# A graph layer on one core: embedding columns inside the message products, features transposed, distances on four row groups

## The chip, the cores and the metric

The kernel runs on 1 core of one Trainium2 chip. The metric is device time in microseconds (us) of one execution. All data is f32.

## What is computed

The input is `x`, 32 graphs of 512 nodes with 256 channels, and `adj`, 32 masks of 512x512 zeros and ones. After a layer norm and a relu (`h`), one graph layer is applied and added to `x`:

```python
h = jnp.maximum(_layernorm(x), 0.0)
# convolution branch
hc = relu(bn1(conv1x1(h)));  x_conv = relu(bn2(conv17(hc)) + h)
# graph branch
s = h @ w_se.T + b_se                          # 3 numbers for each node
sq = jnp.sum(s * s, axis=-1)
dist = sq[:, :, None] + sq[:, None, :] - 2.0 * jnp.einsum('bnd,bmd->bnm', s, s)
A = jnp.exp(-dist) * adj
msg = relu(h @ w_msg.T + b_msg)                # 256 channels
x_nmp = jnp.einsum('bnm,bmd->bnd', A, msg)
# a gated unit on both branches
gi = concat([x_conv, x_nmp]) @ w_ih.T + b_ih;  gh = h @ w_hh.T + b_hh
r, z = sigmoid(gi_r + gh_r), sigmoid(gi_z + gh_z);  n = tanh(gi_n + r * gh_n)
out = x + (1 - z) * n + z * h
```

The change touches the graph branch alone: `s`, `dist` and `msg`.

## The kernel before

The kernel is written in a tile framework that orders the instructions of each engine itself, from the order in which the code issues them and from its own estimates; waits come from the tiles that instructions share. The order of the code therefore sets the order of the engines only roughly. Graphs are called b (0 to 31), in two groups of 16 (GB = 16). HT[b] is `h` of one graph with channels on the partitions, 128 x 2 x 512.

The program runs through these stages, with their place in the profiled execution:

- 0 to 249 us, "first" and "gen": layer norm, transposes (`phT`) and the 1x1 convolution (`pc`, L266) of graphs 0 to 15; the weights of the 17-tap convolution go to frequencies (`pw`, L216: products of 17 rows on four row groups of the array, each in its own PSUM bank). The weights of the graph branch and of the gates are fetched in `load_weights`, on ACT's DMA queue.
- 249 to 628 us, "nodes": the graph branch of graphs 0 to 15. In between lie 40 frequency products (`py`, L309), two for each even b and three for each odd b, two of them behind `affinity`, the third at the end of the pass.
- 628 to 735 us: "first" of graphs 16 to 31.
- 735 to 1390 us, "rest": gates of graphs 0 to 15, with the second 40 frequency products.
- 1390 us to the end, "nodes" and "rest" together: graph branch and gates of graphs 16 to 31. While the gates of graph b run, the graph branch of b + 1 is worked in between.

The graph branch of one graph consists of these functions:

- `embed`: `ps` (L329), a product of 96 weight columns with HT[b], computes the three numbers of each node three times, on partitions 0, 32 and 64. Four ACT instructions (L332 to L335) add the bias, double or square, and write the tiles `sl` and `sr` (96 x 512), of which 32 rows each hold a constant -1.
- `message`: `pm` (L345), 128 nodes by 256 channels for each of four chunks of nodes, two chunks to a bank; DVE adds the bias (L348), ACT takes the relu (L349).
- `affinity`: for each of four chunks a product `pd` (L357) of 96 rows, which gives -dist at once; ACT takes the exponential `e` (L359); PE transposes the mask into `pa` (L362); DVE multiplies both into `A` (L363).
- `aggregate`: `pn` (L371), the product of `A` and `msg`; DVE copies it out (L373).

The gates are `pg` with the sigmoid `rz` (L426), `pgh`, `pgi` (L411) and `n` (L438); `po` (L453) transposes back. Each matrix product of f32 is two instructions in the trace, and a transpose is one; all PSUM tiles come from one pool of eight banks. The loop of the last stage, in the code's order:

```python
load_nodes(b + 1); load_rest(b + 1, False)
embed(b + 1)
message(b + 1)
gates_rz(b)
affinity(b + 1)
gate_n(b)
aggregate(b + 1)
freq_to_windows(b + 1)
finish(b)
```

## Time and profile before

| | |
|---|---|
| runs | 2270.57, 2271.43, 2273.3 us; median 2271.43 us |
| the profiled execution | 2272.12 us, of which the span of the trace is 2270.3 us |
| granted TensorE clock, mean | 0.979 |
| busy: PE, DVE, ACT | 97%, 33%, 26% of the span |
| the 16 graphs of the "nodes" stage | 379 us |
| bytes moved | 308.89 MB, 136 GB/s on average |

Times in the profile are in us unless marked ns. PE is TensorE's matrix product, PEld its weight load, DVE VectorE, ACT ScalarE, POOL GpSimd, SP SyncE; SPq and ACTq are their DMA queues. A row of a group names its source line, engine, operation, what it writes and reads, the shapes and the count; behind the bar stand busy time and the mean of one in ns, then the idle time of the engine ahead of it and what ended it. In rows in order of time, the first number is the start and the second the time until the last of the row's instructions has ended; the ends of matrix products overlap the next one's start, so that their pace is read from start to start.

### The profile page before, as it was taken

The numbers are of one execution on the slowest core, as the hardware profiler recorded it, in microseconds if no ns is written. First come the engines' busy times: TensorE is split into PE (matmuls) and PEld (weight loads), VectorE is DVE, ScalarE is ACT, GpSimd is POOL, SyncE is SP. The second block draws the span as 40 slices with busy tenths as digits, with TensorE's granted clock in tenths as the row PEclk, the third lists the DMA queues.
The fourth block names the chain that finished last, engine by engine and source line by source line (L and its number), as shares of the span: only waits on it lengthen the run. The fifth ranks groups of instructions, "written<-read, shape, count | busy, mean of one in ns | idle before, by whom it ended". The sixth has DMA issues, their size and how long they took to land.

```text
span 2270.3 us, 20711 instructions
## 1 busy us (share of the span) xinstructions
PE 2197.3 (97%) x8000; PEld 1316.4 (58%) x8000; DVE 744.6 (33%) x1416; ACT 596.5 (26%) x946; POOL 93.0 (4%) x119
## 2 busy tenths in 40 slices
PE   5888999999999999999999999999999999999998
PEld 4556666666688555555555554555555555555554
DVE  5556422223277122321321222223322222222323
ACT  1333333333234211111111111322222322222221
POOL 1000100000011000000000000000000000000000
PEclk7888999999999999999999999999999999999999
DMA  7878665665554453464464443222222222222210
GB/s 207 275 228 264 202 235 197 221 217 198 199 190 153 119 181 118 148 194 126 129 187 132 147 143 81 71 75 64 73 64 76 78 73 64 64 64 64 64 37 19
DMA packets 207650, 308.89 MB, mean 136 GB/s; under 512 B 11713, under 2 KB 158145, under 8 KB 207553
## 3 DMA queue, kind: packets, MB, share of 16 engines
q1 hardware_dynamic: 193152, 272.93, 39.2%
q10 hardware_dynamic: 14401, 34.65, 4.1%
q8 instruction: 63, 1.03, 0.2%
q14 instruction: 34, 0.28, 0.0%
HBM read 202.68 MB, written 104.86 MB: 135 GB/s over the span
## 4 chain that ended last, share of the span: by engine, by line
PE 91%; DVE 4%; DMA 3%; issue 1%; POOL 1%; ACT 0%; SPq 0%; DVEq 0%; POOLq 0%; ACTq 0%
PE pg L411 29%; PE pgi L411 10%; PE pn L371 10%; PE py L309 9%; PE pc L401 5%; PE pd L357 5%; PE pgh L411 5%; PE pm L345 5%; PE pc L266 4%; PE pa L362 2%; PE ps L329 2%; PE px L280 2%; PE pw L216 1%; PE po L453 1%; DMA x<-in_x_dram 1%; DVE stats L235 1%
## 5 line engine op out<-in xcount | busy, mean ns | idle before, releaser
L411 PE MATMUL pg<-nmp,wih 128*128 128x512 f32 x512 | 240.8, 592 | 0.0
L411 PE MATMUL pg<-hT,whh 128*128 128x512 f32 x512 | 240.6, 592 | 0.0
L411 PE MATMUL pg<-xconv,wih 128*128 128x512 f32 x512 | 240.6, 592 | 0.0
L426 ACT ACTIVATE rz<-pg,brz 128x512 f32<-128x512 f32 x128 | 87.9, 687 | 555.3 <-PE pg L411 549.8
L371 PE MATMUL pn<-A,msg 128*128 128x512 f32 x512 | 224.9, 592 | 0.0
L363 DVE TENSOR_TENSOR A<-e,pa 128x512 f32<-128x512 f32 x128 | 86.6, 687 | 396.6 <-ACT e L359 395.6
L314 DVE COPY y<-py 128x256 f32<-128x256 f32 x78 | 33.1, 425 | 416.4 <-PE py L309 407.8
L411 PEld LDWEIGHTS pg<-xconv,wih 128*128 128x128 f32 x512 | 97.3, 190 | 122.5 <-issue 122.5
L411 PEld LDWEIGHTS pg<-nmp,wih 128*128 128x128 f32 x512 | 97.2, 190 | 122.0 <-issue 121.7
L371 PEld LDWEIGHTS pn<-A,msg 128*128 128x128 f32 x512 | 97.2, 190 | 122.0 <-issue 114.0
L411 PEld LDWEIGHTS pg<-hT,whh 128*128 128x128 f32 x512 | 97.0, 190 | 108.6 <-issue 104.3
L309 PE MATMUL py<-wt,xf 128*128 128x256 f32 x640 | 152.7, 381 | 0.0
L438 ACT ACTIVATE n<-n,vec 128x512 f32<-128x512 f32 x64 | 46.2, 722 | 329.3 <-DVE n L437 329.3
L401 PEld LDWEIGHTS pc<-back,yt 120*128 120x128 f32 x1024 | 121.9, 195 | 18.4 <-issue 18.3
L309 PEld LDWEIGHTS py<-wt,xf 128*128 128x128 f32 x640 | 121.8, 191 | 16.4
L266 PE MATMUL pc<-w,hT 128*128 128x256 f32 x512 | 130.7, 413 | 0.4 <-DVE hT L254 0.4
L357 PE MATMUL pd<-sr,sl 96*128 96x512 f32 x256 | 131.1, 593 | 0.0
L401 PE MATMUL pc<-back,yt 120*128 120x80 f32 (+1 forms) x1024 | 120.6, 277 | 3.2 <-DMA yt<-yd 3.2
L266 PEld LDWEIGHTS pc<-w,hT 128*128 128x128 f32 x512 | 105.0, 209 | 29.0 <-ACT wst L225 12.2
L411 PE MATMUL pgh<-hT,whh 128*128 128x512 f32 x256 | 120.3, 592 | 0.0
L411 PE MATMUL pgi<-nmp,wih 128*128 128x512 f32 x256 | 120.3, 592 | 0.0
L411 PE MATMUL pgi<-xconv,wih 128*128 128x512 f32 x256 | 120.3, 592 | 0.0
(78 smaller groups left out, 2364.7 us busy)
## 6 DMA issues: line engine op xcount, KB each, us to landing
wt<-wd SPq DMA_DIRECT2D x160, 384.0 KB
x<-in_x_dram SPq DMA_DIRECT2D x64, 512.0 KB
adj<-in_adj_dram SPq DMA_DIRECT2D x32, 1024.0 KB
wd<-wst SPq DMA_DIRECT2D x64, 480.0 KB
yd<-y ACTq DMA_DIRECT2D x80, 384.0 KB
yt<-yd SPq DMA_DIRECT2D x64, 480.0 KB
hT<-hd SPq DMA_DIRECT2D x48, 512.0 KB
hd<-hT SPq DMA_DIRECT2D x32, 512.0 KB
```

What stands on the lines that cost most here:

```text
L266: nc.tensor.matmul(p[:, j, :], HT[b][:, ic, c * P : (c + 1) * P], w1[:, ic, :], start=(ic == 0), stop=(ic == DC - 1))
L280: nc.tensor.matmul(p[:, j * 2 * L : (j + 1) * 2 * L], H1[b][:, c0 + j, ic * P : (ic + 1) * P], fwd, start=True, stop=True)
L309: nc.tensor.matmul(dst, v[:, ic, :], wt[:, ic, k, :], start=(ic == 0), stop=(ic == DC - 1))
L329: nc.tensor.matmul(p[:96, :], wse[:, ic, :], HT[b][:, ic, :], start=(ic == 0), stop=(ic == DC - 1))
L345: nc.tensor.matmul(p[:, j, :], HT[b][:, ic, c * P : (c + 1) * P], wmsg[:, ic, :], start=(ic == 0), stop=(ic == DC - 1))
L357: nc.tensor.matmul(pd, SL[b % 2][:, m], SR[b % 2], start=True, stop=True)
L363: nc.vector.tensor_mul(A[b][:, mc, :], e, pa)
L371: nc.tensor.matmul(p, MSG[b][:, mc, dc * P : (dc + 1) * P], A[b][:, mc, :], start=(mc == 0), stop=(mc == NC - 1))
L401: nc.tensor.matmul(p[:, t0:t1], YT[b][w][:, oc * P : (oc + 1) * P], back[:, u0 : u0 + t1 - t0], start=(w == 0), stop=(w == W - 1), skip_gr ...
L411: nc.tensor.matmul(p, w, v, start=(i == 0), stop=(i == len(terms) - 1))
L426: nc.scalar.activation(RZ[b][:, g, :], p, AF.Sigmoid, bias=brz[:, g : g + 1], scale=1.0)
L438: nc.scalar.activation(n, n, AF.Tanh, bias=b_in[:, i : i + 1], scale=1.0)
```

## The change

Three things are done together.

The embedding weights become three more columns of the message weights. `ps` is gone; `pm` has 259 columns instead of 256, with a bank of its own for each chunk, so that `s` comes out with nodes on the partitions (`st`). The bias is added by DVE, apart for the three columns and the 256.

`embed` now runs behind `message`. DVE squares `st` and writes four copies of the nine features of each node into `fl` and `fr` (four places of 32 columns). PE transposes these with four instructions for each side (`psl`, `psr`), and ACT copies them into `sl` and `sr` (128 x 512), where the features stand on partitions 0, 32, 64 and 96.

`affinity` issues its four products `pd` behind each other, each on nine rows of another row group, into four banks; the exponentials, the transposes of the mask and the products with it follow.

In the loops `message(b + 1)` and `embed(b + 1)` swap around `aggregate(b)` in the "nodes" stage, and `embed(b + 1)` stands behind `gates_rz(b)` in the last stage. Six small DMAs ahead of `load_weights` on ACT's queue go, and two come into it.

```diff
-    for q in range(3):
-        nc.scalar.dma_start(wse[:, :, 32 * q : 32 * q + NS], w_seT.rearrange("(c p) t -> p c t", p=P))
-        nc.scalar.dma_start(bse[32 * q : 32 * q + NS, :], b_se)
...
-    wmsg = consts.tile([P, DC, D], FP, name="wmsg")
-    bmsg = consts.tile([P, D], FP, name="bmsg")
+    wmsg = consts.tile([P, DC, D + NS], FP, name="wmsg")
+    bmsg = consts.tile([P, D + NS], FP, name="bmsg")
...
+    fl = consts.tile([P, NC, 4, 32], FP, name="fl")
+    fr = consts.tile([P, NC, 4, 32], FP, name="fr")
...
-    def embed(b):
-        p = bank(f"ps_{b}")
-        for ic in range(DC):
-            nc.tensor.matmul(p[:96, :], wse[:, ic, :], HT[b][:, ic, :], start=(ic == 0), stop=(ic == DC - 1))
...
     def message(b):
...
+                p = bank(f"pm_{b}_{c}")
                 for ic in range(DC):
-                    nc.tensor.matmul(p[:, j, :], HT[b][:, ic, c * P : (c + 1) * P], wmsg[:, ic, :],
+                    nc.tensor.matmul(p[:, : D + NS], HT[b][:, ic, c * P : (c + 1) * P], wmsg[:, ic, :],
                                      start=(ic == 0), stop=(ic == DC - 1))
-            nc.vector.tensor_add(m, p, bmsg[:, None, :].to_broadcast([P, h, D]))
+                nc.vector.tensor_add(ST[b][:, 0, c, :], p[:, D : D + NS], bmsg[:, D:])
+                nc.vector.tensor_add(m[:, j, :], p[:, :D], bmsg[:, :D])
             nc.scalar.activation(m, m, AF.Relu)
 
+    def embed(b):
+        st = ST.pop(b)
+        nc.vector.tensor_mul(st[:, 1], st[:, 0], st[:, 0])
+        s1, s2 = (st[:, k, :, None, :].to_broadcast([P, NC, 4, NS]) for k in range(2))
+        nc.vector.tensor_copy(fl[:, :, :, :NS], s1)
+        nc.vector.tensor_copy(fl[:, :, :, NS : 2 * NS], s2)
+        nc.vector.tensor_scalar(fr[:, :, :, :NS], s1, 2.0, None, op0=ALU.mult)
+        nc.vector.tensor_scalar(fr[:, :, :, 2 * NS : 3 * NS], s2, -1.0, None, op0=ALU.mult)
+        for side, f, name in ((SL, fl, "sl"), (SR, fr, "sr")):
+            p = bank(f"p{name}_{b}")
+            for c in range(NC):
+                nc.tensor.transpose(p[:, c * P : (c + 1) * P], f[:, c].rearrange("p g k -> p (g k)"), ident)
+            t = side[b] = pools["nodes"].tile([P, N], FP, tag=name, name=f"{name}_{b}", bufs=2)
+            nc.scalar.copy(t, p)
+
     def affinity(b):
...
+        pd = [bank(f"pd_{b}_{mc}") for mc in range(NC)]
+        for mc in range(NC):
+            rows = slice(32 * mc, 32 * mc + 3 * NS)
+            nc.tensor.matmul(pd[mc], sl[rows, mc * P : (mc + 1) * P], sr[rows, :], start=True, stop=True)
         for mc in range(NC):
             m = slice(mc * P, (mc + 1) * P)
-            pd = bank(f"pd_{b}_{mc}")
-            nc.tensor.matmul(pd, SL[b % 2][:, m], SR[b % 2], start=True, stop=True)
```

What the engines then execute, in order, at three places. First PE in the last stage, between the end of the gates' `pg` of graph 16 and its `pgh`, with the affinity of graph 17 in between. Before:

```order
L411 MATMUL pg_3_7442<-xconv_7362,wih 128x512 x2
L357 MATMUL pd_0_7451<-sr_149,sl_147 128x512
L362 MATMUL pa_0_7455<-ident,adj_7389 128x128 x4
L357 MATMUL pd_1_7461<-sr_149,sl_147 128x512
L362 MATMUL pa_1_7465<-ident,adj_7389 128x128 x4
L357 MATMUL pd_2_7471<-sr_149,sl_147 128x512
L362 MATMUL pa_2_7475<-ident,adj_7389 128x128 x4
L357 MATMUL pd_3_7481<-sr_149,sl_147 128x512
L362 MATMUL pa_3_7485<-ident,adj_7389 128x128 x4
L411 MATMUL pgh_0_7492<-hT_16_7278,whh 128x512 x2
```

And now, on PE at the same place:

```order
L411 MATMUL pg_3_7789<-xconv_7478,wih 128x512 x2
L344 MATMUL psl_7802<-ident,fl 128x128 x4
L344 MATMUL psr_7809<-ident,fr 128x128 x4
L355 MATMUL pd_0_7817<-sr_7814,sl_7807 128x512
L355 MATMUL pd_1_7818<-sr_7814,sl_7807 128x512
L355 MATMUL pd_2_7819<-sr_7814,sl_7807 128x512
L355 MATMUL pd_3_7820<-sr_7814,sl_7807 128x512
L362 MATMUL pa_0_7827<-ident,adj_7734 128x128 x4
L362 MATMUL pa_1_7835<-ident,adj_7734 128x128 x4
L362 MATMUL pa_2_7843<-ident,adj_7734 128x128 x4
L362 MATMUL pa_3_7851<-ident,adj_7734 128x128 x4
L411 MATMUL pgh_0_7858<-hT_16_7602,whh 128x512 x2
```

The transposes `psl` and `psr` now stand directly ahead of `pd`, which reads their copies; nothing of another graph stands between them. On ACT at this place there were the last sigmoid and then the exponentials; now the two copies lie between:

```order
L426 ACTIVATE rz_7764<-pg_3_7789,brz 128x512
L346 COPY sl_7807<-psl_7802 128x512
L346 COPY sr_7814<-psr_7809 128x512
L359 ACT_TABLE_LOAD
L359 ACTIVATE e_0_7825<-pd_0_7817 128x512
L359 ACTIVATE e_1_7833<-pd_1_7818 128x512
```

The copies thus wait for the sigmoid of the last `pg`, and the table load and the exponentials for the copies. Second, PE in the "nodes" stage, around the aggregation of graph 0. Before:

```order
L329 MATMUL ps_1930<-hT_1_1897,wse 96x512 x2
L371 MATMUL pn_0_1938<-A_1856,msg_1841 128x512 x4
L371 MATMUL pn_1_1944<-A_1856,msg_1841 128x512 x4
L345 MATMUL pm_0_1951<-wmsg,hT_1_1897 128x256 x4
L345 MATMUL pm_2_1958<-wmsg,hT_1_1897 128x256 x4
L357 MATMUL pd_0_1967<-sr_149,sl_147 128x512
L362 MATMUL pa_0_1971<-ident,adj_1899 128x128 x4
```

And now, on PE:

```order
L326 MATMUL pm_3_1957<-wmsg,hT_1_1906 128x259 x2
L371 MATMUL pn_0_1964<-A_1865,msg_1822 128x512 x4
L371 MATMUL pn_1_1970<-A_1865,msg_1822 128x512 x4
L344 MATMUL psl_1981<-ident,fl 128x128 x4
L344 MATMUL psr_1988<-ident,fr 128x128 x4
L355 MATMUL pd_0_1997<-sr_1993,sl_1986 128x512
L355 MATMUL pd_1_1998<-sr_1993,sl_1986 128x512
```

`message` went ahead of `pn`, and the transposes stand between `pn` and `pd`. It is so in 8 of the 15 passes; in the 7 passes of odd b the third product stands between, as here on PE in the next pass:

```order
L371 MATMUL pn_1_2106<-A_1996,msg_1939 128x512 x4
L344 MATMUL psl_2117<-ident,fl 128x128 x4
L344 MATMUL psr_2124<-ident,fr 128x128 x4
L299 MATMUL py_4_2136<-wt_4_2132,both_4_2137 128x256 x2
L299 MATMUL py_4_2136<-wt_4_2132,xf_215 128x256 x2
L299 MATMUL py_0_4_2139<-wt_4_2132,xf_215 128x256 x2
L355 MATMUL pd_0_2150<-sr_2129,sl_2122 128x512
```

There one whole product moved in between the transposes and their reader. Third, ACT at the start of the program, behind the DMA of `back`. Before:

```order
L162 DMA bse<-in_b_se_dram 3x1
L172 DMA wmsg<-in_w_msgT_dram 128x2x256
L173 DMA bmsg<-in_b_msg_dram 128x256
L174 DMA whh<-in_w_hhT_dram 128x2x768
L225 ACT_TABLE_LOAD
L225 COPY wst_0_0_282<-pw_0_0_286 120x512
L175 DMA wih<-in_w_ihT_dram 128x4x768
```

And now, on ACT:

```order
L162 DMA wmsg<-in_w_msgT_dram 128x2x256
L163 DMA wmsg<-in_w_seT_dram 128x2x3
L164 DMA bmsg<-in_b_msg_dram 128x256
L165 DMA bmsg<-in_b_se_dram 128x3
L166 DMA whh<-in_w_hhT_dram 128x2x768
L167 DMA wih<-in_w_ihT_dram 128x4x768
L215 ACT_TABLE_LOAD
```

The weights `wih` are now fetched ahead of the first copy instead of behind it.

## The prediction, made before the changed kernel ran

> **What bounds the kernel now.** I read the page's busy times first, then the stretches of the two stages in which the graph branch runs.

> ```profile
> PE 2197.3 (97%) x8000; PEld 1316.4 (58%) x8000; DVE 744.6 (33%) x1416; ACT 596.5 (26%) x946; POOL 93.0 (4%) x119
> ```

> ```profile
> core 0: us, PE busy (x) PEld busy (x) DVE busy (x) ACT busy (x) POOL busy (x), PEclk, DMA share, GB/s
> ...
> 249.00:628.00 379.00, 379.00 (x1441) 247.86 (x1440) 104.77 (x167) 123.98 (x202) 28.28 (x39) 1.00 0.62 212
> ...
> 1442.00:2250.00 808.00, 808.00 (x2628) 427.71 (x2627) 223.71 (x331) 219.29 (x305) 0.00 (x0) 1.00 0.22 63
> ```

> In "nodes" (249 to 628) and in the last stage (from 1442) PE is busy for the whole stretch at a granted clock of 1.00, with ACT and DVE under a third. Each microsecond of PE work taken out there is a microsecond of the span, and each wait that PE newly takes is one lost. Next I read the rows in order of time for PE, for the pace from start to start.

> ```profile
> 1465.66 1.88 PE L411 MATMUL pg<-xconv,wih 128*128 128x512 f32 x4
> 1467.38 1.02 PE L357 MATMUL pd<-sr,sl 96*128 96x512 f32 x2
> 1468.24 0.60 PE L362 MATMUL pa<-ident,adj 128*128 128x128 f32 x4
> 1468.68 1.02 PE L357 MATMUL pd<-sr,sl 96*128 96x512 f32 x2
> ...
> 1472.58 1.88 PE L411 MATMUL pgh<-hT,whh 128*128 128x512 f32 x4
> ...
> 1494.15 1.88 PE L329 MATMUL ps<-hT,wse 128*96 128x512 f32 x4
> 1495.87 3.62 PE L345 MATMUL pm<-wmsg,hT 128*128 128x256 f32 x16
> 1499.32 1.88 PE L411 MATMUL pg<-hT,whh 128*128 128x512 f32 x4
> ...
> 1519.92 1.02 PE L357 MATMUL pd<-sr,sl 96*128 96x512 f32 x2
> ```

> So one `pd` takes 0.86 us (1467.38 to 1468.24), four transposes 0.44, the affinity of a graph 5.20 (1467.38 to 1472.58, four times 1.30), `ps` 1.72 and `pm` 3.45. All of it is back to back, and a pass of the last stage takes 52.5 (1467.38 to 1519.92).

> **The change, part by part, for one graph, times 32.**

> `ps` goes: 1.72 x 32 = -55.0.

> `pm` has 259 columns for 256: 3.45 x 3/256 = 0.04, x 32 = +1.3. An odd width is not in the trace; if it cost a tenth of `pm`, it would be 11 us, and no gain is to be had there. I take the proportion, since the widths 256 (3.45 for 16) and 512 (1.72 for 4, 0.43 each) go by columns: 0.216 and 0.430 for one.

> The eight transposes `psl`, `psr` are like those of the mask: 2 x 0.44 = 0.88, x 32 = +28.2.

> The four `pd` on four row groups are a form that the trace has already, in the frequency weights of the first stage: 17 rows, 512 columns, four row groups, four banks.

> ```profile
> 44.51 1.99 PE L216 MATMUL pw<-w2p,taps 17*120 17x512 f32 x16
> 46.43 1.78 PE L266 MATMUL pc<-w,hT 128*128 128x256 f32 x7
> ...
> 83.84 1.99 PE L216 MATMUL pw<-w2p,taps 17*120 17x512 f32 x16
> 85.76 3.72 PE L266 MATMUL pc<-w,hT 128*128 128x256 f32 x16
> ...
> 83.84:85.76 1.92, 1.92 (x16) 0.72 (x16) 0.69 (x1) 0.59 (x1) 1.00 0.97 320
> ```

> The last line is the stretch of the second burst: its granted clock is 1.00, and its DMA share 0.97 at 320 GB/s. Sixteen instructions, which is two sets of four products, take 1.92 us both times, with full-array work before and behind: 0.96 for a set. Against 4 x 0.86 = 3.44 this is -2.48, x 32 = -79.4. The ends of the range are no overlap (3.44, no gain) and one row group's own two passes (0.86, -82.6); the `pw` rows differ from `pd` only in 17 rows for 9 and 120 outputs for 128, so I take theirs. [...]

> The sum of PE's work is -55.0 + 1.3 + 28.2 - 79.4 = -104.9 us.

> **The new waits.** `pd` now waits for ACT's copies of transposes that stand just ahead of it in PE's queue, and behind `pd` the whole queue waits. Nothing of before shows this round trip, so I build it from its pieces.

> ```profile
> 1467.58 0.69 ACT L426 ACTIVATE rz<-pg,brz 128x512 f32<-128x512 f32 x1 [4.46 <-PE pg L411]
> 1468.29 1.28 ACT L359 ACT_TABLE_LOAD   x1
> ...
> L310 ACT COPY y<-py 128x512 f32<-128x512 f32 x80 | 46.9, 586 | 118.9 <-PE py L309 118.9
> ...
> 228.58 0.63 ACT L270 ACTIVATE h<-h 128x512 f32<-128x512 f32 x1 [1.61 <-DVE h L269]
> ...
> 229.26 1.66 PEld L280 LDWEIGHTS px<-fwd,h 128*128 128x128 f32 x12 [0.52 <-ACT h L270]
> ```

> ACT starts 0.20 after PE's last column slot (1467.38 to 1467.58); PE resumes 0.05 after ACT (229.21 to 229.26); a copy of a bank takes 0.59. In the last stage, counted from the end of `pg`: the sigmoid runs from 0.20 to 0.89, the copy of `sl` to 1.49, that of `sr` to 2.08, `pd` starts at 2.13, and the transposes filled the first 0.88. PE stands still for 1.25. In 15 graphs (17 to 31) that is 18.8. The DVE work of `embed` is hidden by `pg` and costs nothing: the chain of waits has it as one piece of 20.6 us in each pass.

> ```profile
> 1446.94 20.60 PE pg L411 x48
> ```

> In "nodes" ACT is idle there: `sl` is copied from 0.64 to 1.23, `sr` to 1.82, `pd` at 1.87, a stall of 1.0. It falls in the 8 passes where nothing stands between: 8.0. In the 7 others a product covers it:

> ```profile
> 484.66 3.62 PE L345 MATMUL pm<-wmsg,hT 128*128 128x256 f32 x16
> 488.11 1.03 PE L309 MATMUL py<-wt,both 128*128 128x256 f32 x4
> 488.98 1.89 PE L309 MATMUL py<-wt,xf 128*128 128x256 f32 x8
> 490.70 1.02 PE L357 MATMUL pd<-sr,sl 96*128 96x512 f32 x2
> ...
> 502.80 7.03 PE L371 MATMUL pn<-A,msg 128*128 128x512 f32 x16
> 509.67 3.62 PE L345 MATMUL pm<-wmsg,hT 128*128 128x256 f32 x16
> 513.12 1.02 PE L357 MATMUL pd<-sr,sl 96*128 96x512 f32 x2
> ```

> The product lasts 2.59 (488.11 to 490.70), more than the 1.0. The DVE work of `embed` lies beside `pn`, 6.87 us (502.80 to 509.67); if that cover were gone, these small instructions would add to the stall. How much shows at the two starts, graph 0 and graph 16, where `embed` follows `message` at once.

> ```profile
> L238 DVE TENSOR_SCALAR rstd<-mv 128x4 f32<-128x4 f32 x32 | 5.4, 170 | 1.1
> ...
> L314 DVE COPY y<-py 128x256 f32<-128x256 f32 x78 | 33.1, 425 | 416.4 <-PE py L309 407.8 <-DMA adj<-in_adj_dram 8.7
> ```

> Behind `pm` come an add of three columns, one of 256 (0.42) and four small ones, 0.17 each as an estimate from the row of 128x4: 0.20 + 0.17 + 0.42 + 0.68 = 1.5 until the first transpose, then the round trip of 1.0: 2.5 for graph 0, and 2.0 for graph 16, where six transposes `po` stand in between.

> Stalls: 18.8 + 8.0 + 2.5 + 2.0 = +31.3 us. Below they could be less only if ACT were faster than its own rows; above, a further 0.5 us in each of 25 places would be 13.

> What goes off ACT and onto DVE is hidden: ACT loses four instructions of `ps` and gains two copies for each graph; DVE's message add splits in two and gets eight small ones, some 2.5 us for each graph, where DVE is busy for 105 of 379 us. `pd` of one graph needs four banks at a time; the exponentials of before start as `pd` ends and each takes 0.60, so that `pgh`, which stands 2.7 us behind the start of `pd` (0.96 + 1.75), finds the first bank free at 1.28 + 0.60 = 1.9.

> At the start ACT issues its weights earlier:

> ```profile
> 8.54 0.44 ACTq L161 DMA_DIRECT2D wse<-in_w_seT_dram  x1
> ...
> 11.05 0.40 ACTq L172 DMA_DIRECT2D wmsg<-in_w_msgT_dram  x1
> ...
> 14.76 13.61 DMA wih<-in_w_ihT_dram
> 28.39 0.32 SPq L204
> ...
> 30.57 4.12 DMA x<-in_x_dram
> ```

> The chain there runs from the landing of `wih` (28.37) to SP's next loads and to `x` of graph 1. `wih` would be issued some 3.7 us earlier, at about 11, but its bytes share the queues with the same neighbours, and SP meets the wait two loads earlier in its own order, so that about 1.2 us more of issues follow it. I take -1, between -4 and +4.

> **The sum.** The profiled execution took 2272.1 us (0.7 above the median of 2271.4): 2272.1 - 104.9 + 31.3 - 1 = 2197.5, of which the median's place takes off 0.7: about 2197 us, 3.3% faster.

> **The rivals.**

> - *The row groups run in turn.* Then `pd` keeps 3.44 and 79.4 comes back: 2276, slower by 0.2%; without that gain the change loses 4.9 us, since the stalls eat what `ps` and the transposes leave (55.0 - 1.3 - 28.2 = 25.5 against 31.3, and -1). It decides when a set takes over 3.4 us. Against it stand both `pw` rows.
> - *The transfers hold the "nodes" stage.* DMA is busy 0.62 there at 212 GB/s; shortened by 42 us (16 x 3.28, less the stalls of 10.5) it must move the same bytes at 238. The burst of `pw` above ran beside 320 GB/s, and PE waited for no load in "nodes" before; but the loads of adjacency and of products share one queue, each behind its own release. If the stage kept its 379 us, the time would be 2197 + 42 = 2239.
> - *PE waits for the exponentials.* Four banks filled in 0.96 us are emptied at 0.60 each behind a table load of 1.28: 3.7 us, where PE has 2.7 to fill. If `pgh` had to wait for all, 1.0 x 16 would be added: 2213. The order of the banks speaks against it. [...]
> - *No stall.* If the copies were hidden, 31.3 less: 2166. Against it: PE's queue is in order and the rows stand directly behind each other.
> - *Twice the stall*, by longer waits between engines than these rows show: 2228.

> **How the numbers follow.** My forecast has a chance of 0.64, and its own range is 2184 to 2212, made of -4 to +4 at the start, 13 for the stalls, and -3 to +5 for the sets (or 11 for an odd width). Transfers 0.10, exponentials 0.09, twice the stall 0.08, row groups in turn 0.05, no stall 0.04. The range of 2182 to 2238 holds the first, third and fifth case wholly and part of the second; left out are 0.04 below and about 0.12 above. A difference of 0.2% (4.5 us) is about what a measurement of this kernel can tell from no change. Faster by more than that: all but the row groups in turn and mishaps together, 0.94; within it 0.02; slower 0.04.

> **What would show it.** Right: no group `ps`; four `pd` from first start to `pa` in about 1.0 us; `pm` at 3.5; eight transposes at 0.9; PE idle ahead of `pd` for 1.0 to 1.3 us in some 23 graphs, released by ACT's copy; "nodes" at about 337 us, the last 15 passes at about 50.5 instead of 52.5 us each (-3.28 + 1.25). Wrong: `pd` starting 0.4 to 0.9 apart; PE waiting ahead of `pm` or `pa` for a transfer, or ahead of `pgh` for an exponential; waits of other places in the first 249 us.

## The result, and the profile after

The changed kernel takes 2209.64 us (median of four runs) beside 2271.0 us of the kernel before on the same chip; the ratio is 0.9725 [0.9696, 0.9754], 2.75% faster. The forecast was 2197, so 12 to 13 us of the expected gain are missing. The profiled execution took 2209.7 us, its span is 2207.9 us against 2270.3 us: 62.4 us less. Where the runs of a kernel fall into a faster and a slower group, the times below are those of the faster one.

The page's busy times, and the same two stretches as before (the columns are those shown there):

```profile
PE 2117.3 (96%) x8128; PEld 1295.9 (59%) x8128; DVE 772.2 (35%) x1765; ACT 544.2 (25%) x882; POOL 92.9 (4%) x119
```

```profile
254.00:596.00 342.00, 334.51 (x1503) 235.40 (x1503) 118.88 (x343) 97.70 (x170) 28.23 (x39) 0.99 0.66 235
1412.00:2190.00 778.00, 765.01 (x2687) 414.76 (x2686) 236.09 (x495) 194.72 (x276) 0.00 (x0) 1.00 0.22 65
```

PE's busy time fell by 80.0 us and the span by only 62.4: PE now stands still in both stages (342.00 against 334.51, 778.00 against 765.01). "Nodes" moves its bytes at 235 GB/s instead of 212 and no wait for a transfer stands in it. The groups of the new instructions (count, busy time, mean ns of one, then the idle time ahead and what ended it) name the new waits:

```profile
L355 PE MATMUL pd<-sr,sl 9*128 9x512 f32 x256 | 38.3, 668 | 20.2 <-ACT sr L346 20.2
L344 PE MATMUL psl<-ident,fl 128*128 128x128 f32 x128 | 19.8, 278 | 2.7 <-DVE fl L338 2.7
L326 PE MATMUL pm<-wmsg,hT 128*128 128x259 f32 x512 | 117.4, 382 | 0.0
```

PE's rows in order of time, one pass of the last stage:

```profile
1434.57 0.60 PE L344 MATMUL psl<-ident,fl 128*128 128x128 f32 x4
1435.01 0.60 PE L344 MATMUL psr<-ident,fr 128*128 128x128 f32 x4
1436.47 1.14 PE L355 MATMUL pd<-sr,sl 9*128 9x512 f32 x8 [0.87 <-ACT sr L346]
1437.55 1.97 PE L362 MATMUL pa<-ident,adj 128*128 128x128 f32 x16
1439.35 1.88 PE L411 MATMUL pgh<-hT,whh 128*128 128x512 f32 x4
...
1486.92 1.14 PE L355 MATMUL pd<-sr,sl 9*128 9x512 f32 x8 [0.87 <-ACT sr L346]
```

The four `pd` take 1.08 us together (1436.47 to 1437.55), `psl` and `psr` 0.44 each, and a pass takes 50.45 (1436.47 to 1486.92) where it took 52.5. From the last column of `psr` (1435.01 + 0.43) to `pd` PE stands still for 1.03. `pgh` follows `pa` without a wait. ACT's rows of the same place:

```profile
1434.77 0.69 ACT L426 ACTIVATE rz<-pg,brz 128x512 f32<-128x512 f32 x1 [4.46 <-PE pg L411]
1435.36 0.58 ACT L346 COPY sl<-psl 128x512 f32<-128x512 f32 x1
1435.82 0.60 ACT L346 COPY sr<-psr 128x512 f32<-128x512 f32 x1
```

The sigmoid, the two copies and PE's release stand in the forecast's order. Each starts some 0.1 before the one ahead of it has ended, which the forecast's adding up of durations left out.

### The profile page after: what moved, and what is told of

Read it like the earlier page. It is cut to its first block, busy times and chain, and to the rows that moved or that the text cites. A ratio compares the mean times of both kernels' runs of the same rounds, so it can differ in the third digit from the quotient of the medians.

```text
span 2207.9 us, 21176 instructions
## 1 busy us (share of the span) xinstructions
PE 2117.3 (96%) x8128; PEld 1295.9 (59%) x8128; DVE 772.2 (35%) x1765; ACT 544.2 (25%) x882; POOL 92.9 (4%) x119
## 3 DMA queue, kind: packets, MB, share of 16 engines
q8 instruction: 64, 1.05, 0.2%
## 4 chain that ended last, share of the span: by engine, by line
PE 90%; DVE 4%; DMA 2%; ACT 2%; issue 1%; POOL 1%; SPq 0%; ACTq 0%; DVEq 0%; POOLq 0%
PE pg L411 30%; PE pn L371 10%; PE pgi L411 10%; PE py L299 9%; PE pc L401 5%; PE pgh L411 5%; PE pm L326 5%; PE pc L256 5%; PE pa L362 3%; PE px L270 2%; PE pd L355 2%; PE pw L206 2%; PE po L453 1%; DVE h L259 1%; DVE x L232 1%
## 5 line engine op out<-in xcount | busy, mean ns | idle before, releaser
L411 PE MATMUL pg<-nmp,wih 128*128 128x512 f32 x512 | 240.8, 593 | 0.0
L411 PE MATMUL pg<-hT,whh 128*128 128x512 f32 x512 | 240.7, 592 | 0.0
L411 PE MATMUL pg<-xconv,wih 128*128 128x512 f32 x512 | 240.7, 593 | 0.0
L371 PE MATMUL pn<-A,msg 128*128 128x512 f32 x512 | 226.0, 595 | 0.0
L426 ACT ACTIVATE rz<-pg,brz 128x512 f32<-128x512 f32 x128 | 87.9, 687 | 558.3 <-PE pg L411 558.3
L363 DVE TENSOR_TENSOR A<-e,pa 128x512 f32<-128x512 f32 x128 | 82.6, 684 | 392.9 <-ACT e L359 389.9
L304 DVE COPY y<-py 128x256 f32<-128x256 f32 x78 | 33.1, 425 | 415.7 <-PE py L299 415.7
L411 PEld LDWEIGHTS pg<-xconv,wih 128*128 128x128 f32 x512 | 97.5, 190 | 122.3 <-issue 122.3
L411 PEld LDWEIGHTS pg<-nmp,wih 128*128 128x128 f32 x512 | 97.4, 190 | 121.8 <-issue 121.6
L371 PEld LDWEIGHTS pn<-A,msg 128*128 128x128 f32 x512 | 97.8, 191 | 115.8 <-issue 114.8
L411 PEld LDWEIGHTS pg<-hT,whh 128*128 128x128 f32 x512 | 97.2, 190 | 108.6 <-issue 104.1
L411 PE MATMUL pgh<-hT,whh 128*128 128x512 f32 x256 | 120.4, 593 | 0.0
L411 PE MATMUL pgi<-nmp,wih 128*128 128x512 f32 x256 | 120.3, 593 | 0.0
L411 PE MATMUL pgi<-xconv,wih 128*128 128x512 f32 x256 | 120.3, 593 | 0.0
L326 PE MATMUL pm<-wmsg,hT 128*128 128x259 f32 x512 | 117.4, 382 | 0.0
```

The costliest lines, as they stand in the source:

```text
L326: nc.tensor.matmul(p[:, : D + NS], HT[b][:, ic, c * P : (c + 1) * P], wmsg[:, ic, :], start=(ic == 0), stop=(ic == DC - 1))
L363: nc.vector.tensor_mul(A[b][:, mc, :], e, pa)
L371: nc.tensor.matmul(p, MSG[b][:, mc, dc * P : (dc + 1) * P], A[b][:, mc, :], start=(mc == 0), stop=(mc == NC - 1))
L411: nc.tensor.matmul(p, w, v, start=(i == 0), stop=(i == len(terms) - 1))
L426: nc.scalar.activation(RZ[b][:, g, :], p, AF.Sigmoid, bias=brz[:, g : g + 1], scale=1.0)
```

## The experiments

**The row groups, by using fewer of them.**

```diff
-            rows = slice(32 * mc, 32 * mc + 3 * NS)
+            rows = slice(0, 3 * NS)                                # one group
+            rows = slice(32 * (mc % 2), 32 * (mc % 2) + 3 * NS)    # two groups
```

One row group: 

> The changed kernel with all four distance products on row group 0 (rows 0 to 8) instead of one on each group; nothing else changes. If the gain of the products comes from their running side by side, a set goes from the 1.08 us of the changed kernel to 4 x 0.86 = 3.44: +2.36 x 32 = 75, about 2285 us, slower than the kernel before. If it comes from nine rows instead of 96, or from issuing the four behind each other, nothing changes: 2210.

Two row groups: 

> The four distance products alternate between row groups 0 and 1. If groups overlap and one group is serial, a set takes two rounds of two: 1.72 plus the 0.2 that the set of four has over its own 0.86, about 1.9 us, +0.8 x 32 = 26, about 2236 us. If neighbours only overlap when all four groups are in use, 3.4 us and 2285.

Two groups took 2241.6 us (three runs between 2241.5 and 2246.5), ratio 0.9859 [0.9832, 0.9886]; one group took 2340.15 and 2344.28 us, far above both expectations. PE's rows of two groups, then of one group in the second pass of the last stage, with the stretches of that place, and in one of the later passes:

```profile
1504.82 1.99 PE L355 MATMUL pd<-sr,sl 9*128 9x512 f32 x8 [0.87 <-ACT sr L346]
1506.74 1.97 PE L362 MATMUL pa<-ident,adj 128*128 128x128 f32 x16
```

```profile
1502.47 5.14 PE L355 MATMUL pd<-sr,sl 9*128 9x512 f32 x8 [0.86 <-ACT sr L346]
1507.54 3.68 PE L362 MATMUL pa<-ident,adj 128*128 128x128 f32 x16
1511.01 1.23 PE L411 MATMUL pgh<-hT,whh 128*128 128x512 f32 x2
```

```profile
1500.00:1503.00 3.00, 2.14 (x11) 1.23 (x10) 0.00 (x0) 2.21 (x4) 0.00 (x0) 1.00 0.00 0
1503.00:1506.00 3.00, 3.00 (x7) 1.38 (x6) 0.00 (x0) 1.91 (x3) 0.00 (x0) 0.76 0.00 0
1506.00:1510.00 4.00, 4.00 (x14) 2.50 (x14) 1.07 (x2) 0.52 (x1) 0.00 (x0) 0.50 0.00 0
```

```profile
1832.09 3.70 PE L355 MATMUL pd<-sr,sl 9*128 9x512 f32 x8 [0.86 <-ACT sr L346]
1835.72 3.59 PE L362 MATMUL pa<-ident,adj 128*128 128x128 f32 x16
```

A set of four products takes 1.08 on four groups and 1.92 on two. On one it takes 3.62 to 3.71 in 24 of the 32 passes, and up to 5.96 in the eight others, where the clock is low within the set; the 5.07 of the first rows is one of these. So the products of different row groups do run beside each other, and products of one group run in turn: 4 x 0.86 is 3.44. With one group the granted clock (third number from the end, a mean over the stretch) falls to 0.50, in the second pass within the set and through `pa`, in the later passes behind the set, so that `pa` takes 3.3 to 3.5 from its start to the next product instead of 1.80. That fall was in neither expectation.

**Why the clock falls with one group.** Two kernels keep the products in turn, and change one thing each. In the first, each product runs over all 128 rows, which hold the features four times, and the exponential takes a quarter of the result. In the second, the products stay on nine rows, and four `pa` stand behind each.

```diff
-            rows = slice(32 * mc, 32 * mc + 3 * NS)
-            nc.tensor.matmul(pd[mc], sl[rows, mc * P : (mc + 1) * P], sr[rows, :], start=True, stop=True)
+            nc.tensor.matmul(pd[mc], sl[:, mc * P : (mc + 1) * P], sr, start=True, stop=True)
...
-            nc.scalar.activation(e, pd[mc], AF.Exp)
+            nc.scalar.activation(e, pd[mc], AF.Exp, scale=0.25)
```

All rows: 

> Each distance product runs over all 128 rows, which hold the features four times, and the exponential divides by four; the four products stand in a row as in the changed kernel. Theory A, the low clock of the run with one row group comes from so few rows at work (nine for some 3 us): here all rows work, the set takes 4 x 0.86 = 3.44 us at the full clock, the pa behind it 1.8 us, total 2209 + 32 x (3.44 - 1.08) = 2285. Theory B, it comes from four products in a row after the pause, whatever their rows: about 2340 to 2390 as with one row group.

```diff
         for mc in range(NC):
             m = slice(mc * P, (mc + 1) * P)
+            rows = slice(0, 3 * NS)
+            nc.tensor.matmul(pd[mc], sl[rows, m], sr[rows, :], start=True, stop=True)
```

Nine rows, with `pa` in between: 

> All four products on row group 0 as in the run with one row group, but each followed by its four pa, as before the change. Theory A (few rows at work for some 3 us bring the clock down): each product is over after 0.86 us and full rows follow, so the clock holds and the time is 2285 as above, or a little above it. Theory C, any product of nine rows lowers the clock whatever its neighbours: the low clock stays, 2340 to 2390.

All rows took 2280.91 us, ratio 1.0043 [1.0025, 1.0062]; nine rows with `pa` in between took 2466.94 us, ratio 1.0853 [1.0828, 1.0878]. First the rows of all 128 rows, and its last stage as a whole:

```profile
1470.02 3.70 PE L354 MATMUL pd<-sr,sl 128*128 128x512 f32 x8 [0.87 <-ACT sr L346]
1473.56 1.91 PE L361 MATMUL pa<-ident,adj 128*128 128x128 f32 x16
```

```profile
1442.00:2250.00 808.00, 794.98 (x2691) 431.31 (x2690) 237.80 (x497) 196.29 (x275) 0.00 (x0) 1.00 0.21 63
```

Then nine rows with `pa` in between:

```profile
1622.36 1.12 PE L356 MATMUL pd<-sr,sl 9*128 9x512 f32 x2 [0.87 <-ACT sr L346]
1623.41 0.66 PE L361 MATMUL pa<-ident,adj 128*128 128x128 f32 x4
1624.00 1.92 PE L356 MATMUL pd<-sr,sl 9*128 9x512 f32 x2
```

```profile
1622.30:1625.00 2.70, 2.64 (x8) 1.06 (x8) 0.69 (x1) 1.89 (x3) 0.00 (x0) 0.85 0.00 0
1625.00:1632.00 7.00, 7.00 (x15) 2.48 (x13) 1.37 (x2) 1.20 (x2) 0.00 (x0) 0.50 0.00 0
```

With all rows at work the set takes 3.54 us at a clock of 1.00, with the same pause of 0.87 ahead and the same four products in turn; only at graphs 0 and 16 it takes longer (5.24 and 5.55; the clock is 0.54 and then 0.60 in it at graph 0). So in the other passes the pause and the four products didn't bring the clock down by themselves; with nine rows on one group it fell to 0.50. The pause has a share, which the kernel with one group shows. It stands ahead of 25 of the 32 sets there, and the clock falls in or behind each of these. Ahead of the seven others a whole `py` stands in its place, and in five of them the clock stays at 1.00, as in these rows of that kernel:

```profile
461.90 3.70 PE L355 MATMUL pd<-sr,sl 9*128 9x512 f32 x8
465.53 1.97 PE L362 MATMUL pa<-ident,adj 128*128 128x128 f32 x16
```

With `pa` in between, both expectations missed: Theory C had the low clock right, but the time came out 77 us above its upper end. The transposes in between didn't hold the clock. It is low in at least seven of the passes, two of them without a pause (from 600.87 and 658.34, where a product late in the set takes 2.00 instead of 1.05), and for longer: the mean clocks, 0.912 over 2473.6 us here, 0.954 over 2338.4 with the four in a row and 0.977 over 2277.6 with all rows, make it, at a grant of 0.50, an estimated 10 us of low clock for each graph over that with all rows, where the four in a row have 3. That this comes from the same few-row products being spread over a longer time is a guess. "Few rows for some 3 us" of the first theory is right in its first half and wrong in its second, since here the first product is over after 1.05 us and the clock is low some 2 us later (0.85 to 1625.00, then 0.50). Two things stay open: nine rows and one row group always came together, and what stood in between were only transposes, no other product of full rows. On four groups 36 rows work, and the clock stays at 1.00 in the steady passes.

These runs also price the change without its row groups. With one bank after the other and all rows at work, the remaining parts (`ps` gone, features by nodes, transposes, waits) make the kernel slower than before by 0.43%. The whole gain, 2280.9 - 2209.6 = 71 us, is the row groups'. From the sets alone it would be 32 x (3.54 - 1.08) = 79; in the profiled executions the first stage, which varies by itself (below), was 4.8 us shorter with all rows (249.62).

**The waits, by other work between the transposes and `pd`.** `embed` is called one product group earlier, ahead of the last `pg` in `gates_rz` and of the second `pn` in `aggregate`:

```diff
-    def aggregate(b):
+    def aggregate(b, between=lambda: None):
...
+            if dc == 0:
+                between()
...
-    def gates_rz(b):
+    def gates_rz(b, between=lambda: None):
...
+            if g == 2 * DC - 2:
+                between()
```

> The transposes of the features move one product group earlier: between the third and fourth pg in the last stage, and between pn_0 and pn_1 in the first nodes stage. If the stall is the round trip over ACT, it goes: 15 x 1.03 and 8 x 0.9 us, 22 us, about 2187. If ACT's copies are late for another reason (queued behind the sigmoid, or waiting for banks), or PE then waits elsewhere, the time stays at 2205 to 2210.

It took 2185.66 us, ratio 0.9613 [0.9588, 0.9638], 24.0 less than the changed kernel's first median. PE's rows of the last stage:

```profile
1476.28 0.60 PE L344 MATMUL psr<-ident,fr 128*128 128x128 f32 x4
1476.72 1.88 PE L413 MATMUL pg<-hT,whh 128*128 128x512 f32 x4
...
1480.16 1.88 PE L413 MATMUL pg<-xconv,wih 128*128 128x512 f32 x4
1481.96 1.14 PE L355 MATMUL pd<-sr,sl 9*128 9x512 f32 x8
```

```profile
L355 PE MATMUL pd<-sr,sl 9*128 9x512 f32 x256 | 38.3, 669 | 1.4 <-ACT sr L346 1.4
```

`pg` of 5.2 us stands where PE waited; `pd` starts 0.08 behind it (1480.16 + 1.72). The idle time ahead of `pd`, 20.2 us in the changed kernel, is 1.4 here, that of graphs 0 and 16. Counted from the last column of `psr`, each of the 23 waits that are gone was 0.16 longer than the profile's idle time (1.03 for 0.87), which makes 18.8 + 3.7 = 22.5 of the 24.0 us. The two kernels ran on different chips; by their ratios to the kernel before, and with the repeat of the changed kernel below, the difference is 21 to 25 us. Within that, the waits lay on the path one for one.

**The two starts.** At graphs 0 and 16 `embed` follows `message` at once, and there the granted clock is low too (0.50 from 262.70 to 266.20 us and from 1390.80 to 1399.00 in the changed kernel). This kernel, over and above the last one, moves frequency products ahead of and behind the transposes of graph 0, and `freq_to_windows` (`pc`) in two halves around those of graph 16.

```diff
+                product(pw, 0, 0, xf)
                 embed(0)
+                product(pw, 0, 1, xf)
...
-        embed(GB)
         affinity(GB)
         aggregate(GB)
-        freq_to_windows(GB)
```

with `freq_to_windows(GB, lambda: embed(GB))` ahead of `affinity(GB)`. 

> As cover, and at graph 0 two frequency products, at graph 16 the return to windows, stand between message, embed and affinity, so that PE has work during the DVE chain. If the low granted clock behind these two places (0.50 for some 5 to 9 us) comes from PE standing still there, both the idle 1.7 and 2.7 us and the slow stretches of about 3 and 5 us go: 12 us below cover, about 2175. If the clock falls there for another reason, only the idle time goes: about 2182.

It took 2184.45 us, ratio 0.9594 [0.9568, 0.9621]. The same kernel, timed again later beside others: 

> The version with the transposes one product group earlier and other products between them and the distance products at graphs 0 and 16 too, timed again beside the two others: 2183 to 2186, some 25 below the changed kernel, from stalls that are gone (about 22) and the low clock at graphs 0 and 16 that is gone (about 4).

 It then took 2181.95 us, ratio 0.9597 [0.9583, 0.9611]. Graph 0 of the changed kernel, and its clock:

```profile
254.39 3.66 PE L326 MATMUL pm<-wmsg,hT 128*128 128x259 f32 x16
259.01 0.66 PE L344 MATMUL psl<-ident,fl 128*128 128x128 f32 x4 [0.96 <-DVE fl L338]
...
260.83 1.95 PE L355 MATMUL pd<-sr,sl 9*128 9x512 f32 x8 [0.73 <-ACT sr L346]
262.71 3.67 PE L362 MATMUL pa<-ident,adj 128*128 128x128 f32 x16
```

```profile
259.00:262.70 3.70, 2.96 (x16) 1.24 (x16) 0.05 (x1) 1.32 (x3) 0.00 (x0) 0.77 1.07 370
262.70:266.20 3.50, 3.50 (x21) 3.49 (x18) 1.93 (x3) 2.28 (x4) 0.00 (x0) 0.50 0.50 156
```

Graph 0 in the repeat of the changed kernel:

```profile
257.22 4.98 PE L326 MATMUL pm<-wmsg,hT 128*128 128x259 f32 x16
263.15 0.65 PE L344 MATMUL psl<-ident,fl 128*128 128x128 f32 x4 [0.96 <-DVE fl L338]
...
264.97 1.14 PE L355 MATMUL pd<-sr,sl 9*128 9x512 f32 x8 [0.73 <-ACT sr L346]
```

Graph 16 of the changed kernel:

```profile
1390.85 1.12 PE L344 MATMUL psl<-ident,fl 128*128 128x128 f32 x4 [1.76 <-DVE fl L338]
1393.49 2.09 PE L355 MATMUL pd<-sr,sl 9*128 9x512 f32 x8 [0.68 <-ACT sr L346]
1395.51 3.68 PE L362 MATMUL pa<-ident,adj 128*128 128x128 f32 x16
1398.98 8.08 PE L371 MATMUL pn<-A,msg 128*128 128x512 f32 x16
```

And graph 16 with work in between, in the second run of that kernel:

```profile
1382.05 0.66 PE L344 MATMUL psl<-ident,fl 128*128 128x128 f32 x4 [1.34 <-DVE fl L338]
...
1384.81 1.14 PE L355 MATMUL pd<-sr,sl 9*128 9x512 f32 x8
1385.88 1.97 PE L362 MATMUL pa<-ident,adj 128*128 128x128 f32 x16
1389.11 7.13 PE L371 MATMUL pn<-A,msg 128*128 128x512 f32 x16 [1.26 <-DVE A L363]
```

At graph 16 `pd` takes 2.09 without the work and 1.14 with it, `pa` 3.68 and 1.97, `pn` 8.08 and 7.13. The three differences add up to about 3.6 us for the low clock, and the slower `psl` and `psr` make it 4.5. The four profiles of kernels without this work and with four row groups all have the low clock there, from `pm` of graph 16 to that of graph 17 in 24.5 to 26.2 us; the two with it don't, and take 21.4. What went is the low clock alone. PE still stands idle there, 1.34 ahead of `psl` and, new, 1.26 ahead of `pn`, which waits for `A`: together 2.60, where `po`, `psl` and `pd` had 0.29 + 1.76 + 0.68 = 2.73.

At graph 0 the idle time of 0.96 + 0.73 is gone, but that the work keeps the clock up is not shown. In the six profiles of kernels with four row groups the clock is low either in `pd` and `pa` (two) or already in `pm` (four). Both profiles with the work are among the four, as is the repeat without it above, where `pm` is slow and `pd` is not. The "nodes" stage is 335.5 in the profile of the kernel above and 331.6 with the work; about 2 of these 3.9 us are this difference of place. The medians of 2185.66 against 2184.45 and 2181.95, with intervals that overlap, don't settle a gain over the kernel with only the first cover; the expected 2175 was too low, since it counted the idle time at graph 16 as gone and the low clock at graph 0 as cured. Both beat the kernel before and the changed one.

**The first stage.** It lasted 249.26 us before and 254.39 after, though the changed code ahead of it is only loads and clears. This kernel puts the old loads and their clears back, unread:

```diff
+    for q in range(3):
+        nc.scalar.dma_start(wse[:, :, 32 * q : 32 * q + NS], w_seT.rearrange("(c p) t -> p c t", p=P))
+        nc.scalar.dma_start(bse[32 * q : 32 * q + NS, :], b_se)
```

Loads put back: 

> The changed kernel with the seven loads and clears of the old embedding weights put back at the start (nothing reads them). Theory A, the first stage is 3 to 6 us longer because those loads, now gone, had set the order in which the startup transfers land: the first stage goes back to 249 to 250 us and the total to about 2205. Theory B, the first stage's length is set by where the low clock falls in its first 75 us, and those loads do nothing: it stays at 252 to 256 us, and the total at about 2209 to 2210.

The changed kernel again: 

> The changed kernel unaltered, as the measure for the run beside it. Theory A (order of the startup transfers): first stage 254 to 255 us again. Theory B (where the low clock falls, by chance): anywhere from 249 to 256 us, with another stretch of low clock between 20 and 75 us than the first profile's 57 to 75 us. Total 2209 to 2210 by either.

The kernel before, twice more: 

> The kernel before, unaltered, for the length of its first stage (249.3 us in its first profile, against 251.7 to 257.2 in six of the changed kind). If the first stage's length is chance of the clock: between 249 and 257 us here. If the change lengthens it by itself: within 1 us of 249.3.

 and 

> As the run beside it, a second look at the first stage of the kernel before: between 249 and 257 us by chance of the clock, or within 1 us of 249.3 by the change.

With the loads back it took 2206.91 us, ratio 0.9706 [0.9688, 0.9724]; the changed kernel beside it 2208.07 us, ratio 0.9707 [0.9693, 0.9721]: no difference. The first stage lasted 251.71 us with the loads and 257.22 without, but 251.82 in another kernel without them. The kernel before took 248.92 and 251.15 us for it in its two further profiles (2267.45 and 2271.32 us). One stretch tells the long ones from the short ones, from 57 to 75 us; the rows are of the kernel before (its first profile), the changed kernel, and the changed kernel again:

```profile
57.00:75.00 18.00, 16.91 (x93) 11.17 (x91) 11.66 (x27) 9.78 (x20) 1.01 (x1) 0.97 0.80 262
```

```profile
57.00:75.00 18.00, 17.98 (x81) 11.95 (x81) 8.37 (x19) 6.96 (x14) 0.13 (x1) 0.64 0.68 224
```

```profile
57.00:75.00 18.00, 17.97 (x73) 12.37 (x73) 6.54 (x11) 6.29 (x12) 0.00 (x0) 0.58 0.75 238
```

Four profiles of changed kernels, with a clock of 0.58 to 0.72 there, took 254.4 to 257.2; the six others (0.91 to 0.97) took 249.6 to 252.9; the three of before (0.93 to 0.97) 248.9 to 251.2. Theory A is out as the main cause. What stays open: whether the low clock's place, which none of three profiles of before shows, is chance alone, and some 2 us between the groups of high clock.

## Why the prediction was right, and where it was off

*Right.* The direction, and the mechanism in all its steps: `ps` gone, `pm` by its columns (3.50 from 1460.92 to 1464.42 in the order of time, forecast 3.49), transposes 0.44 a side, sets of `pd` side by side, 25 waits for ACT's copy. A last pass takes 50.45 (forecast 50.5), and two passes of "nodes" 42.17 (forecast 41.87). The rivals of transfers, exponentials, no stall and twice the stall are out by the rows above; the products in turn, with all rows at work, gave 2281, which the forecast put at 2276.

*Off.* The forecast of 104.9 us less work for PE compares with 86.7 us less busy time in the two stages of the graph branch (44.2 and 42.5). Of the 18 us between them the sets of `pd` are 4, low clock at graphs 0 and 16 is 8, and 4 are waits that the profile counts as busy, 0.16 in each of 25. The change of each stage, forecast and measured, between the two profiled executions:

| stage | forecast | measured | why |
|---|---|---|---|
| first (to graph 0) | -1 | +5.13 | low clock at 57 to 75 us |
| "nodes" | -42.0 | -36.75 | graph 0: low clock 3.3, set 0.2, wait 0.5 shorter; 15 slower passes, 2.2 |
| "first" of graphs 16 to 31, to the first `pg` | 0 | -3.99 | varies by itself |
| "rest" | 0 | +0.04 | |
| last stage | -31.6 | -26.83 | graph 16: low clock 4.5, longer waits and set 1.2; passes 0.9 shorter |
| sum | -74.6 | -62.40 | |

The term "start of the program, -1, between -4 and +4" was looked for in the order of DMAs, and the size lay in the clock; +5.13 is outside its bounds. The stage of graphs 16 to 31 lasted 128.4 in the first profile of before and 123.5 and 125.7 in the two further ones, so that its -4.0 isn't the change's. It is luck that these two terms, 6 us too long and 4 us too short, nearly cancel; with the first alone the time would have been about 2214, above the forecast's own range.

The terms of 2.5 and 2.0 for graphs 0 and 16 counted PE's standing still (1.7 and 2.4 in the rows above) and left out what follows from it. From `pm` of graph 0 to `pm` of graph 1 it is 16.94 here (254.39 to 271.33) and 14.94 in the repeat (257.22 to 272.16), with the same waits of 0.96 and 0.73. The repeat has low clock too, but in `pm`: from there to `psl` it takes 5.93 instead of 4.62, and from `psl` to the next `pm`, at a clock of 1.00, 9.01 instead of 12.32. So the low clock in `pd` and behind it costs 3.3 us, and that in `pm` 1.3. The waits themselves therefore don't decide it alone. The same waits went with a low clock in `pd` in one execution (1.95) and not in the other (1.14); what else decides was not shown.

The set of `pd`, forecast at 0.96, takes 1.08, and where no wait stands ahead it starts 0.08 late. The step that failed is the halving of a burst of two sets. The 1.92 of the `pw` burst is 2 x 0.86 with 0.20 around it, as the two-group kernel shows (1.92 again, two in turn) and the one-group kernel too (3.62, where 4 x 0.86 is 3.44); one set alone keeps the whole 0.20: 0.86 + 0.20 = 1.06. Over 32 graphs that is 4 us for the set. Against four products in turn the set is 3.44 / 1.08 = 3.2 times as fast. No run shows the +5 for the sets in the forecast's range; what the runs show is the 4 us of this 1.08 in place of 0.96.

The stall of 1.25 in the last stage is 1.03, since ACT's instructions overlap by 0.1 each; over 15 graphs this gives back 3.3. In "nodes" it is 0.89 for 1.0.

## What to carry to other kernels

Where a short product is moved onto row groups, put other work of full rows between what it waits for and itself; here 24 us lay in a call placed one product group too late. A fixed cost around a burst is shared by all that is in the burst, so a burst of two (1.92 here) is not twice a burst of one (1.08). Price a stop of TensorE with the clock that may follow it, and with a spread, since the same stops came with 1.3 us of it at graph 0 in one execution and 3.3 in another.

## What the runs showed of the hardware

In the clock records of two traces, that of the kernel before and that of the changed kernel, the grant is 1.00 or 0.50, nothing in between, and each stretch of 0.50 but the last, which ends behind the program, lasted a whole multiple of 3.41 us: 3.41 to 13.65 before, 3.41 to 17.07 after. A 0.76 in the rows above is a mean over its stretch.
